# A selective scan in two layers: carry columns by transfer, D u by a diagonal matmul, 1/std turned later

## The chip, the cores and the metric

The kernel runs on one core of a Trainium2 chip. Five engines work side by side, each through its own queue of instructions in order: TensorE (matmuls, PE in the profile, with its weight loads as PEld), VectorE (DVE), ScalarE (ACT), GpSimd (POOL) and SyncE (SP), which here only issues transfers. The metric is the device time of one execution in microseconds (us), the median of several runs.

## What is computed

The reference has two layers over an input of 4 x 192 x 128 x 128 floats. Layer 1 (group norm, fractional Fourier transforms, small convolutions) is not touched by the change. Layer 2 takes most of the time. It is a state space block on sequences of 16384 tokens with 192 channels, 4 of them in the batch:

```python
seq = (seq - mu) * lax.rsqrt(var + LN_EPS) * ln_g + ln_b      # layer norm per token
xs, z = jnp.split(einsum('blc,ec->ble', seq, in_proj_w), 2)   # 384 inner channels each
u = silu(conv1d(xs, 4 taps, per channel))
dt, Bm, Cm = split(einsum('bld,kd->blk', u, x_proj_w))        # 16 states
dt = softplus(einsum('blr,dr->bld', dt, dt_proj_w) + dt_proj_b)
h[t] = h[t-1] * exp(dt[t] * A) + (dt[t] * u[t]) * B[t]        # 384 channels x 16 states
y[t] = sum over states (h[t] * C[t]) + u[t] * Dp
out = einsum('bld,cd->blc', y * silu(z), out_proj_w)
```

All in float32. The recurrence over t is what makes the work serial: h at the end of one stretch of tokens is the start of the next.

## The kernel before

Layer 2 (`layer1` in the code, which counts from 0) cuts each sequence into chunks of T = 512 tokens: 32 per batch entry, 128 in all. The 384 inner channels are NJ = 3 tiles (j) of 128 partitions. The 16 states are taken in pairs: 8 pairs per tile, 24 **groups** k = 0 to 23 per chunk (j = k // 8, sg = k % 8). One group is the unit of the main loop:

- VectorE scans two states (`tensor_tensor_scan`, L865), 128 x 512 each, into h. Between the scans it forms products dt u B of later groups (L816).
- ScalarE makes exp(dt A) for states ahead (L796).
- GpSimd multiplies h of the group by C (`hc`, L878), and in 8 of 24 groups also makes dt u B (`db`, L824).
- TensorE adds up hc over the states, three groups later, by turning it: 8 transposes of 128 x 128 into py in PSUM (`sums`, L891).

The tile h has 3 buffers: group k + 3 writes where group k was, so k must have been read by then.

The other work of layer 2 is spread over the groups. `front(n)` is a generator that does for one chunk all that comes ahead of the scans: norm, in-projection, convolution, SiLU, B and C, dt. It is started two chunks ahead, at group 14, and takes one step per group, so that two fronts are always under way: the older one ends at group 23, the newer one begins. A plain `yield` ends a step. What follows `yield MID` is issued between the two scans of that group, what follows `yield LATE` after both. The order of instructions on each engine is thus written out by hand; no scheduler moves them.

In the newer front the layer norm's 1/std per token comes out in columns (tokens on partitions) and is needed in rows. The path runs over these steps, with the group of the chunk in which each is issued:

- group 18, LATE: sums of squares `var` on TensorE (L630)
- group 19, LATE: square root on ScalarE, which needs a table load (L637)
- group 20: reciprocal on VectorE (L639), then its turn on TensorE (L641); between the scans the copy `rows` on ScalarE (L644)
- group 21, LATE: four matmuls on TensorE that spread each row over 96 partitions (`rb`, L649)
- group 22, between the scans: s times 1/std on VectorE (L654)
- group 23: the first in-projection of that front (L660)

The older front issues two in-projections for z among these (L660): one at group 20, ahead of the turn, and one at group 22.

At the end of each group ScalarE copies the last columns of h into `carry` (L876), for the same group of the next chunk. Once per tile j, in group sg = 1, it multiplies u by Dp in place (`skip`, L905). In group sg = 3 TensorE adds that into py by four transposes (`add_skip`, L910), after `sums` of the group three earlier; py has one buffer, which ScalarE empties into yt in group sg = 2 (`evacuate`, L900), so the first `sums` into the new py waits for that copy. yt is turned back (L920), and VectorE multiplies it with silu(z) (`gate`, L925) in group sg = 6.

SyncE issues the loads of B and C, spread over the partitions (`bc`, L770, 1 MB each, 8 per chunk, in groups 19 to 23 and 0 to 2), the store of B and C they are read from (`dbc`, L727), the load of x (L594) and the store of the result (L942).

Of the kernel before, what the change touches and what calls it, by code (L numbers as in the profile page):

```python
# [10 lines left out]
F32 = mybir.dt.float32  # L11
I32 = mybir.dt.int32
BF16 = mybir.dt.bfloat16
AF = mybir.ActivationFunctionType
ALU = mybir.AluOpType
# [12 lines left out]
NJ = DI // 128  # L28
NS = 16
RANK = 12  # L30
T = 512
# [11 lines left out]
def _bc(ap, axis, n):  # L43

    a = ap.unsqueeze(axis)
    shape = list(a.shape)
    shape[axis] = n
    return a.to_broadcast(shape)
# [455 lines left out]
def layer1(tc, xmid, out, st2, w, n_tok=S * S):  # L504

    nc = tc.nc
    B = len(xmid)
    NCHUNK = n_tok // T
    G = 2
# [6 lines left out]
    MID, LATE = "mid", "late"  # L516
    with ExitStack() as ctx:
        def pool(name, bufs, **kw):
            return ctx.enter_context(tc.tile_pool(name=name, bufs=bufs, **kw))

        cp = pool("l1c", 1)
# [13 lines left out]
        def const(name):  # L535
            src = w[name]
            t = cp.tile(list(src.shape), F32, name="c_" + name)
            nc.sync.dma_start(out=t, in_=src)
            return t

        wiT, ln_g, ln_b, xpT, dtT, dtb = (const(k) for k in ("wiT", "ln_g", "ln_b", "xpT", "dtT", "dtb"))
        cw, cb, dp, woT, A = (const(k) for k in ("cw", "cb", "dp", "woT", "A_log"))

        ident = cp.tile([128, 128], F32, name="ident")
# [17 lines left out]
        for m in range(2 * NJ):  # L562
            for t in range(2):
                nc.tensor.matmul(
                    ps[:, m : m + 1], wiT[:, t, m * 128 : (m + 1) * 128], ln_b[:, t : t + 1],
                    start=t == 0, stop=t == 1,
# [5 lines left out]
        nc.scalar.activation(A, A, AF.Exp)  # L572
        nc.vector.tensor_scalar(A, A, -1.0, None, ALU.mult)

        dcw = cp.tile([128, NJ, 4, 128], F32, name="dcw")
        for j in range(NJ):
            for k in range(4):
# [5 lines left out]
        def psum():  # L583
            return ps1.tile([128, 512], F32, name="ps")
# [4 lines left out]
        got = [{} for _ in range(total)]  # L589
# [9 lines left out]
        def front(i):  # L599

            b, ch = divmod(i, NCHUNK)
            g = got[i]
# [25 lines left out]
            for q in range(4):  # L628
                for t in range(2):
                    nc.tensor.matmul(  # L630
                        var[:, q : q + 1], sq[:, t, q * 128 : (q + 1) * 128], ones[0:CH, 0:1],
                        start=t == 0, stop=t == 1,
# [3 lines left out]
            rs = tp.tile([128, 4], F32, name="rs")  # L636
            nc.scalar.activation(rs, var[:, 0:4], AF.Sqrt, bias=eps, scale=1.0 / C)  # L637
            yield
            nc.vector.reciprocal(rs, rs)  # L639
            rt = psum()  # L640
            nc.tensor.transpose(rt[0:4, 0:128], rs, ident)  # L641
            yield MID
            rows = tp.tile([4, 128], F32, name="rows")
            nc.scalar.copy(rows, rt[0:4, 0:128])  # L644
            yield
            yield LATE
            rb = psum()
            for q in range(4):
                nc.tensor.matmul(  # L649
                    rb[0:CH, q * 128 : (q + 1) * 128], sel[:, q, :], rows, start=True, stop=True  # L650
                )
            yield
            yield MID
            nc.vector.tensor_tensor(s, s, _bc(rb[0:CH], 1, 2), ALU.mult)  # L654
            yield

# [25 lines left out]
            u, zs = g["u"], g["zs"] = {}, {}  # L682
# [92 lines left out]
        def dtu_copy(n, j):  # L775

            g = got[n]
            g["dp"] = psd.tile([128, T], F32, name="dp")
            nc.scalar.copy(g["dp"], g["dtu"][j])  # L779
# [19 lines left out]
        def early(i):  # L799

            if i < len(own):
                decay(own[i], scp.tile([128, T], F32, name="da"))

        def decay_there(s):

            if s < len(states) and s not in turns:
                decay(s, psa.tile([128, T], F32, name="op"))

        def product(s):


            if s in turns and states[s][1] % NG != BY_PE:
                n, k, q = states[s]
                g = got[n]
                dbs[s] = psa.tile([128, T], F32, name="op")
                nc.vector.tensor_tensor(dbs[s], g["dp"], g["bc", k % NG][:, 0, q, :], ALU.mult)  # L816
# [36 lines left out]
        def scans(pos, n, k, between):  # L853
            g = got[n]
            j, sg = divmod(k, NG)
            ch = n % NCHUNK
            if k == 0:
                g["carry"] = tp.tile([128, NJ, NS], F32, name="carry")
                g["before"], last["carry"] = last.get("carry"), g["carry"]
            db = g.pop(("db", k), None)  # L860
            h = scp.tile([128, G, T], F32, name="h", bufs=3)
            for q in range(G):
                st = sg * G + q
                s = G * pos + q
                nc.vector.tensor_tensor_scan(  # L865
                    h[:, q, :], das.pop(s), dbs.pop(s) if db is None else db[:, q, :],
                    0.0 if ch == 0 else g["before"][:, j, st : st + 1], ALU.mult, ALU.add,
                )
                product(s + 2)
                decay_there(s + 3)  # L870
                if q == 0:
                    turned_back(s + 3)
                    between()
                if s in turns:
                    early(turns[s] + AHEAD)
            nc.scalar.copy(g["carry"][:, j, sg * G : (sg + 1) * G], h[:, :, T - 1])  # L876
            hc = scp.tile([128, G, T], F32, name="hc", bufs=5)
            nc.gpsimd.tensor_tensor(hc, h, g["bc", sg][:, 1], ALU.mult)  # L878
            g["hc", k] = hc
# [19 lines left out]
            yt = g["yt", j] = op.tile([128, T // 128, 128], F32, name="yt")  # L899
            nc.scalar.copy(yt, g["py", j])  # L900

        def skip(n, j):

            u = got[n]["u"][j]
            nc.scalar.activation(u, u, AF.Identity, scale=dp[:, j : j + 1])  # L905

        def add_skip(n, j):

            for blk in range(T // 128):
                nc.tensor.matmul(  # L910
                    got[n]["py", j][:, blk, :], got[n]["u"][j][:, blk * 128 : (blk + 1) * 128], ident,
                    start=False, stop=False, is_transpose=True, skip_group_check=True,
                )

        def turn(n, j):
# [51 lines left out]
        with tc.manual_schedule():  # L967
            for i in range(min(2, total)):
                load_x(i)
            for _ in front(0):  # L970
                pass
            for sg in range(NG):
                load_bc(0, sg)
            dtu_copy(0, 0)
            inputs(*order[1])
            for at in range(AHEAD):
                early(at)
            for s in range(2):
                product(s)
            decay_there(2)  # L980


            start_front(1)
            for _ in range(NGR - FRONT):
                parts = {MID: [], LATE: []}
                step(fronts, parts)
                go_on(parts[MID] + parts[LATE])
            tails = []
            for pos, (n, k) in enumerate(order):
                j, sg = divmod(k, NG)  # L990
                if k == FRONT:
                    start_front(n + 2)
                if k == NGR - 2 and n + 1 < total:
                    assert len(fronts) == 1 + (n + 2 < total), fronts
                parts = {MID: [], LATE: []}
                step(tails, parts)

                before = n - (j == 0), (j - 1) % NJ
                if pos >= NG and sg == LAG + 3:
                    gate(*before)  # L1000
                if sg == BY_PE - 1:
                    turned_back(G * (pos + 1))
                if pos >= LAG and sg != LAG:
                    sums(*order[pos - LAG])
                if k == EARLY or sg == LAG - 1 and j < NJ - 1:
                    turned(n, NJ - 1 if k == EARLY else j)
                if sg == NG - 3 and pos + 3 < len(order):
                    m, q = order[pos + 3]
                    dtu_copy(m, q // NG)
                step(fronts, parts)  # L1010
                if pos >= NG and sg == LAG + 1:
                    turn(*before)
                if pos + 2 < len(order):
                    inputs(*order[pos + 2])

                def between():
                    go_on(parts[MID])
                    if sg == LAG and j < NJ - 1:
                        scale_pair(n, j)

                scans(pos, n, k, between)
                if pos >= NG and sg == LAG - 1:
                    evacuate(*before)
                go_on(parts[LATE])
                if sg == 1:
                    skip(n, j)
                if k == EARLY:
                    scale_pair(n, NJ - 1)
                if pos >= LAG and sg == LAG:
                    sums(*order[pos - LAG])  # L1030
                    add_skip(n, j)
                if k == LAG + 3 and n:
                    tails.append(finish(n - 1))
                if k == LAG + 8 and n + 2 < total:
                    load_x(n + 2)
                if k >= NGR - BCL and n + 1 < total:
                    load_bc(n + 1, k - (NGR - BCL))
                if k < NG - BCL and n:
                    load_bc(n, k + BCL)
            for at in order[-LAG:]:  # L1040
                sums(*at)
            evacuate(total - 1, NJ - 1)
            turn(total - 1, NJ - 1)
            gate(total - 1, NJ - 1)
            for _ in finish(total - 1):
                pass
# [139 lines left out]
```

## Time and profile before

Three runs took 11835.06 to 11841.85 us, median 11841.73. The profiled execution spans 11838.7 us. Layer 2 begins its chunks at about 1500 us.

| engine | busy us | share | instructions |
|---|---|---|---|
| TensorE | 9907.6 | 84% | 49034 |
| VectorE | 10772.0 | 91% | 11581 |
| ScalarE | 9108.1 | 77% | 17892 |
| GpSimd | 10080.6 | 85% | 4598 |

| what the change touches | busy us | count | mean ns |
|---|---|---|---|
| ScalarE, carry copies (L876) | 563.3 | 3072 | 188 |
| ScalarE, u times Dp (L905) | 278.5 | 384 | 725 |
| TensorE, D u into py (L910) | 300.6 | 1536 | 332 |
| VectorE, reciprocal (L639) | 22.8 | 128 | 178 |

A row of the timeline reads: start in us, duration in us, engine, line, operation, output <- inputs, output shape <- input shape, count of merged instructions, and in brackets the idle time of the engine just ahead with what ended it. Matmuls are pipelined and their ends are modelled, so how fast TensorE goes is better read from start to start. A row of the windows has the stretch, its length, then busy time (and instructions) of PE, PEld, DVE, ACT and POOL, the granted TensorE clock as a share of full speed, the busy share of the DMA engines and the GB/s they moved.

### The profile page before, as it was taken

Reading aid. Unit: us, or ns where it says so; the run is one execution under the profiler, and the core shown is the slowest. Engines: PE = TensorE matmul, PEld = TensorE weight load, DVE = VectorE, ACT = ScalarE, POOL = GpSimd, SP = SyncE. Lnnn points to the kernel's source line nnn. Section 1 sums busy time; section 2 is a strip of 40 time slices with the busy share of each in tenths; the row PEclk is TensorE's granted clock in tenths of the full one; section 3 lists DMA queues with packets and bytes.
Section 4 is the critical chain, followed back from the end, with each engine's and each line's share of the span. In section 5 each row is a group of like instructions: output and inputs, shape, how many; then the busy total and the mean of one; then the engine's idle time right before and its main releaser. Section 6 shows DMA issues by size and latency. Waiting matters only on the chain.

```text
span 11838.7 us, 147015 instructions
## 1 busy us (share of the span) xinstructions
PE 9907.6 (84%) x49034; PEld 6573.6 (56%) x49034; DVE 10772.0 (91%) x11581; ACT 9108.1 (77%) x17892; POOL 10080.6 (85%) x4598
## 2 busy tenths in 40 slices
PE   4777888888888888888888888888888888888887
PEld 2444355555555555555555555555555555555555
DVE  5565589999999999999999999999999999999999
ACT  2322178888888888888888888888888888888887
POOL 0000089999999999999999999999999999999999
PEclk8888689999999999999999999999999999999998
DMA  8787633333333333333333333333333333333332
GB/s 212 211 214 195 179 122 105 118 123 107 115 123 110 113 123 112 111 123 114 109 123 115 108 123 117 106 123 117 106 123 120 103 123 122 102 122 124 102 121 95
DMA packets 503761, 1490.33 MB, mean 126 GB/s; under 512 B 67889, under 2 KB 118774, under 8 KB 502486
## 3 DMA queue, kind: packets, MB, share of 16 engines
q1 hardware_dynamic: 482518, 1418.00, 37.1%
q0 software_dynamic: 13312, 50.34, 1.3%
q10 hardware_dynamic: 7168, 12.59, 0.3%
q8 instruction: 385, 6.31, 0.2%
q14 instruction: 378, 3.10, 0.1%
HBM read 1325.19 MB, written 155.32 MB: 125 GB/s over the span
## 4 chain that ended last, share of the span: by engine, by line
DVE 35%; ACT 27%; issue 23%; PE 9%; POOL 3%; DMA 2%; SPq 0%; ACTq 0%; DVEq 0%; POOLq 0%
DVE h L865 22%; DVE op L816 10%; ACT da L796 8%; ACT L796 4%; POOL hc L878 3%; PE py L891 2%; ACT dbT L840 2%; ACT op L796 2%; PE pr L471 1%; ACT dt L741 1%; PE ps L660 1%; ACT L741 1%; DMA xt<-in_x 1%; ACT xs L622 1%; ACT zs L690 1%
## 5 line engine op out<-in xcount | busy, mean ns | idle before, releaser
L878 POOL TENSOR_TENSOR hc<-h,bc 128x1024 f32<-128x1024 f32 x3072 | 7196.6, 2367 | 344.6 <-DVE h L865 268.9
L865 DVE TENSOR_TENSOR_SCAN h<-da,carry,op 128x512 f32<-128x512 f32 x3968 | 4932.1, 1263 | 1.3 <-DVE rs L639 0.3
L891 PE MATMUL py<-ident,hc 128*128 128x128 f32 x24576 | 3489.0, 291 | 720.1 <-ACT yt L900 679.9
L891 PEld LDWEIGHTS py<-ident,hc 128*128 128x128 f32 x24576 | 3057.4, 151 | 1716.9 <-POOL db L824 673.4
L796 ACT ACTIVATE da<-dt,c_A_log 128x512 f32<-128x512 f32 x4096 | 2806.0, 721 | 138.6 <-DVE h L865 114.2
L865 DVE TENSOR_TENSOR_SCAN h<-op,carry,db 128x512 f32<-128x512 f32 x1984 | 2510.7, 1266 | 101.5 <-ACT op L796 89.6
L824 POOL TENSOR_TENSOR db<-dtu,bc 128x1024 f32<-128x1024 f32 x1024 | 2418.9, 2362 | 5.6 <-DMA bc<-dbc 5.6
L816 DVE TENSOR_TENSOR op<-dp,bc 128x512 f32<-128x512 f32 x3328 | 2230.7, 670 | 33.3 <-ACT dp L779 33.3
L796 ACT ACTIVATE op<-dt,c_A_log 128x512 f32<-128x512 f32 x2048 | 1411.9, 690 | 818.3 <-DVE h L865 816.7
L660 PE MATMUL ps<-s,c_wiT 96*128 96x512 f32 x3072 | 1498.2, 611 | 12.8 <-ACT zs L690 8.2
L678 PE MATMUL ps<-xs,dcw 128*128 128x512 f32 x3072 | 1448.4, 601 | 0.0
L934 PE MATMUL ps<-yg,c_woT 128*96 128x512 f32 x1536 | 710.5, 598 | 190.9 <-DVE xm L940 190.9
L840 ACT ACTIVATE dbT<-ps,bT 128x128 f32<-128x128 f32 x3072 | 826.0, 373 | 0.0
L796 ACT ACT_TABLE_LOAD x636 | 816.0, 1283 | 11.2
L678 PEld LDWEIGHTS ps<-xs,dcw 128*128 128x128 f32 x3072 | 539.9, 193 | 466.5 <-issue 438.8
L660 PEld LDWEIGHTS ps<-s,c_wiT 96*128 96x128 f32 x3072 | 546.8, 199 | 438.9 <-issue 395.3
L477 POOL DMA_DIRECT2D xmid<-xt x64 | 42.6, 666 | 785.5 <-DVE xt L475 779.3
L876 ACT COPY carry<-h 128x2 f32<-128x2 f32 x3072 | 563.3, 188 | 23.1 <-DVE h L865 22.5
L934 PEld LDWEIGHTS ps<-yg,c_woT 128*96 128x96 f32 x1536 | 239.9, 163 | 557.6 <-issue 330.0
L630 PE MATMUL ps<-ones,xs 96*128 96x1 f32 x2048 | 345.5, 299 | 226.9 <-ACT dt L741 222.0
L745 POOL TENSOR_TENSOR dtu<-dt,u 128x512 f32<-128x512 f32 x384 | 476.6, 1268 | 29.1 <-ACT dt L741 29.1
L630 PEld LDWEIGHTS ps<-ones,xs 96*128 96x128 f32 x2048 | 334.6, 255 | 269.3 <-ACT dt L741 261.2
(173 smaller groups left out, 10771.0 us busy)
## 6 DMA issues: line engine op xcount, KB each, us to landing
bc<-dbc SPq DMA_DIRECT2D x1024, 1024.0 KB, 5.4
xt<-in_x SPq DMA_DIRECT2D x192, 768.0 KB, 9.1
xmid<-xt POOLq DMA_DIRECT2D x64, 768.0 KB, 6.7
xm<-xmid SPq DMA_DIRECT2D x128, 384.0 KB, 3.5
out<-xm SPq DMA_DIRECT2D x128, 384.0 KB, 3.0
d<-x ACTq DMA_DIRECT2D x64, 192.0 KB, 7.6
df<-u SPq DMA_DIRECT2D x16, 512.0 KB, 5.2
u<-df SPq DMA_DIRECT2D x16, 512.0 KB, 11.0
```

Of the source, the lines that this page charges most:

```text
L630: nc.tensor.matmul(var[:, q : q + 1], sq[:, t, q * 128 : (q + 1) * 128], ones[0:CH, 0:1], start=t == 0, stop=t == 1,)
L660: nc.tensor.matmul(pp, wiT[:, t, m * 128 : (m + 1) * 128], s[:, t, :], start=t == 0, stop=t == 1)
L678: nc.tensor.matmul(pc, dcw[:, j, k, :], xs[:, j, k : k + T], start=k == 0, stop=k == 3)
L796: nc.scalar.activation(da, got[n]["dt"][j], AF.Exp, scale=A[:, j, st : st + 1])
L816: nc.vector.tensor_tensor(dbs[s], g["dp"], g["bc", k % NG][:, 0, q, :], ALU.mult)
L824: nc.gpsimd.tensor_tensor(db, _bc(g["dtu"][j], 1, G), g["bc", sg][:, 0], ALU.mult)
L840: nc.scalar.activation(t[:, blk, :], g["tu", j][:, blk, :], AF.Identity, scale=g["bT"][:, blk, q : q + 1])
L865: nc.vector.tensor_tensor_scan(h[:, q, :], das.pop(s), dbs.pop(s) if db is None else db[:, q, :], 0.0 if ch == 0 else g["before"][:, j, st ...
L876: nc.scalar.copy(g["carry"][:, j, sg * G : (sg + 1) * G], h[:, :, T - 1])
L878: nc.gpsimd.tensor_tensor(hc, h, g["bc", sg][:, 1], ALU.mult)
L891: nc.tensor.matmul(py[:, blk, :], hc[:, q, blk * 128 : (blk + 1) * 128], ident, start=first, stop=sg == NG - 1 and q == G - 1 and blk == T ...
L934: nc.tensor.matmul(po[0:CH], woT[:, j, t * CH : (t + 1) * CH], g["yg", j], start=j == 0, stop=j == NJ - 1,)
```

## The change

Three edits, all in layer 2:

- The last columns of h go to `carry` by a transfer that SyncE issues, and no longer by a ScalarE copy. The aim is to relieve ScalarE.
- D u comes from one matmul with a diagonal of Dp (`ddp`, made once ahead of the loop) in place of a ScalarE product and a transpose. Two aims: to relieve ScalarE, and to leave u unchanged.
- The reciprocal moves behind the scans of group 20, so that VectorE doesn't stand at it. What follows moves with it: the turn to group 21, ahead of its scans; `rows` between the scans of group 21; `rb` to group 22, ahead of its scans, which puts it behind the older front's in-projection of that group in TensorE's queue; s times 1/std after the scans of group 22. The in-projection of group 23 stays where it was.

```diff
+        ddp = cp.tile([128, NJ, 128], F32, name="ddp")
+        for j in range(NJ):
+            nc.vector.tensor_scalar(ddp[:, j, :], ident, dp[:, j : j + 1], None, ALU.mult)
...
             nc.scalar.activation(rs, var[:, 0:4], AF.Sqrt, bias=eps, scale=1.0 / C)
             yield
+            yield LATE
             nc.vector.reciprocal(rs, rs)
+            yield
             rt = psum()
             nc.tensor.transpose(rt[0:4, 0:128], rs, ident)
             yield MID
             rows = tp.tile([4, 128], F32, name="rows")
             nc.scalar.copy(rows, rt[0:4, 0:128])
             yield
-            yield LATE
             rb = psum()
             for q in range(4):
                 nc.tensor.matmul(
                     rb[0:CH, q * 128 : (q + 1) * 128], sel[:, q, :], rows, start=True, stop=True
                 )
-            yield
-            yield MID
+            yield LATE
             nc.vector.tensor_tensor(s, s, _bc(rb[0:CH], 1, 2), ALU.mult)
...
-            nc.scalar.copy(g["carry"][:, j, sg * G : (sg + 1) * G], h[:, :, T - 1])
+            nc.sync.dma_start(out=g["carry"][:, j, sg * G : (sg + 1) * G], in_=h[:, :, T - 1])
...
-        def skip(n, j):
-
-            u = got[n]["u"][j]
-            nc.scalar.activation(u, u, AF.Identity, scale=dp[:, j : j + 1])
-
         def add_skip(n, j):
 
             for blk in range(T // 128):
                 nc.tensor.matmul(
-                    got[n]["py", j][:, blk, :], got[n]["u"][j][:, blk * 128 : (blk + 1) * 128], ident,
-                    start=False, stop=False, is_transpose=True, skip_group_check=True,
+                    got[n]["py", j][:, blk, :], got[n]["u"][j][:, blk * 128 : (blk + 1) * 128],
+                    ddp[:, j, :], start=False, stop=False, skip_group_check=True,
                 )
...
-                if sg == 1:
-                    skip(n, j)
```

## The prediction

> **What bounds the kernel now.** I read the waits first, then the windows, then the timeline of one chunk, engine by engine.
>
> Of the waits (engine, line, released by: us in total, times, longest) these matter to layer 2:
>
> ```profile
> DVE rs L639 <- ACT rs L637: 292.7, 128, 5.1
> POOL hc L878 <- DVE h L865: 268.9, 136, 18.7
> DVE h L865 <- ACT op L796: 97.1, 148, 2.7
> ```
>
> The windows give busy time per engine in 1000 us of steady layer 2:
>
> ```profile
> 6000.00:7000.00 1000.00, 853.58 (x4437) 581.29 (x4436) 959.38 (x1019) 850.47 (x1691) 967.29 (x437) 0.93 0.35 119
> ```
>
> VectorE is busy 959 us and GpSimd 967 us. A chunk is 80.45 us (L639 starts at 6017.53 and 6097.98), so VectorE idles 3.1 us per chunk and GpSimd 2.5. VectorE's idle time is two waits: 2.23 us for the square root ahead of L639, and 0.7 us for L796. GpSimd's idle time follows from the first: it catches up while VectorE stands. If all waits went, GpSimd would set the pace at 80.45 - 2.5 = 77.9 us.
>
> The timeline round that wait, VectorE:
>
> ```profile
> 6095.07 0.67 DVE L816 TENSOR_TENSOR op<-dp,bc 128x512 f32<-128x512 f32 x1
> 6097.98 0.18 DVE L639 RECIPROCAL rs<-rs 128x4 f32<-128x4 f32 x1 [2.23 <-ACT rs L637]
> 6103.97 0.67 DVE L925 TENSOR_TENSOR yg<-ps,zs 128x512 f32<-128x512 f32 x1
> 6105.73 1.19 DVE L654 TENSOR_TENSOR s<-s,ps 96x1024 f32<-96x1024 f32 x1
> ```
>
> ScalarE, which has no idle time from 6072 to 6098:
>
> ```profile
> 6091.05 0.74 ACT L905 ACTIVATE u<-u,c_dp 128x512 f32<-128x512 f32 x1
> 6094.43 0.57 ACT L900 COPY yt<-py 128x512 f32<-128x512 f32 x1
> 6097.68 0.27 ACT L637 ACTIVATE rs<-ps,eps 128x4 f32<-128x4 f32 x1
> ```
>
> TensorE, from the evacuation of py on:
>
> ```profile
> 6095.14 1.94 PE L891 MATMUL py<-ident,hc 128*128 128x128 f32 x8 [2.72 <-ACT yt L900]
> 6096.88 1.06 PE L910 MATMUL py<-ident,u 128*128 128x128 f32 x4
> 6097.73 1.91 PE L891 MATMUL py<-ident,hc 128*128 128x128 f32 x8
> 6099.44 1.98 PE L660 MATMUL ps<-s,c_wiT 96*128 96x512 f32 x4
> 6101.26 0.28 PE L641 MATMUL ps<-ident,rs 128*4 128x128 f32 x1
> ...
> 6103.64 1.11 PE L649 MATMUL ps<-rows,sel 4*96 4x128 f32 x8
> 6104.68 1.09 PE L891 MATMUL py<-ident,hc 128*128 128x128 f32 x8
> 6105.61 1.88 PE L660 MATMUL ps<-s,c_wiT 96*128 96x512 f32 x4
> 6107.33 1.04 PE L891 MATMUL py<-ident,hc 128*128 128x128 f32 x8
> ```
>
> From 6095.14 to the end of L649 at 6104.75 TensorE has no pause. So a second chain runs beside the first: yt, 9.6 us of TensorE, then L654, which finds its sums ready with 1.0 us to spare.
>
> [...] the eight turns of L891 take 1.74 us to the next start at 6095.14 and 0.93 at 6104.68. [...] here four turns are four records, four f32 matmuls of L649 are eight of like spacing, so I take a factor of two. [...] In the packet records of this trace 4 bytes take 9 ns in the median. [...]
>
> **The change part by part.**
>
> *Carry by transfer.* ScalarE loses 24 copies per chunk; each delays the next instruction by 0.09 us, together 2.2 us. VectorE waited for them 4.2 us in all. New: the h tile is free only when the transfer has landed. Lower bound of landing: 1.6 us (dbc store). Upper: it follows a bc load issued one group earlier, which lands 7.1 us after issue at worst; groups are about 3.3 us apart, so 7.1 + 0.4 issue - 3.3 + 0.2 = 4.4 us. VectorE needs the tile again two groups later, about 6 us. I take no wait. Behind a carry issue in SP's order stand the bc loads: they now start at the end of their group's scans, land some 6 us later, and the earliest reader (L824, after the product hc two groups on) comes about 9 us later: no wait. Transfer engines: 17 packets of about 10 ns, 0.2 us per group beside a DMA share of 0.35.
>
> *D u by a diagonal.* ScalarE loses three L905, 2.2 us per chunk, one of them ahead of yt. TensorE gets four more records three times a chunk: 0.43 us each at full clock, 0.85 at half. The one in group 19 lies on the chain above. Setup of ddp: three small VectorE products, nothing beside 11.8 ms.
>
> *Reciprocal after the scans of group 20.* VectorE gets there 3.5 us after 6095.65, the square root is over by 6098: the 2.23 us go.
>
> *The rest of the turn one group later.* This is where it is decided. L649 now stands behind L891 of group 19 and the older front's L660: 0.93 + 1.72 us more of TensorE ahead of it, and L654 comes after both scans of group 22.
> - TensorE: L905 and six carry copies gone before yt give 0.7 + 0.5 = 1.2 us, so the chain starts at 6093.9. It lasts 9.6 + 0.85 + 0.93 + 1.72 = 13.1 us and ends at 6107.0.
> - VectorE is free of the group before at 6095.65. Then scan, product, scan, product (3.53), reciprocal 0.1, two scans 2.36, gate 0.58, two scans 2.37: it reaches L654 at 6104.6.
> - New wait: 2.4 us. The same working for the four other neighbouring chunks (reciprocals at 6017.5, 6178.4, 6259.4, 6339.8; chains of 9.1 without a wait for VectorE, 10.35, 9.2, 9.86) gives 1.65, 3.2, 1.8, 2.8. Mean 2.36: what differs is how long the half clock lasts.
> - TensorE's pause ahead of the chain shrinks from about 1.8 to 1.0 us, so the clock may come back sooner. An estimate: 0.3 to 0.6 us less half clock, worth half of it, 0.15 to 0.3. I take 2.15 us, range 1.2 (the clock soon back) to 3.0 (half clock throughout).
>
> Behind L654 stand the scans of group 23, so the wait costs VectorE its full length. The 0.7 us for L796 stay: ScalarE starts that stretch from the dp copy, which waits for a VectorE product.
>
> Sum per chunk: -2.23 + 2.15 = -0.1 us; over 127 chunks -10 us, and a few more for carry waits: **11,830 us**, no change that can be told.
>
> **Rivals.**
> 1. *The wait goes and GpSimd becomes the bound.* For: GpSimd needs only 77.9 us, and ScalarE is relieved of 4.4 us per chunk. Against: even at full clock the chain is about 10.6 us, from 6093.9 to 6104.5, just where VectorE arrives; it needs a TensorE that never slows there. If so: 2.2 to 2.5 us in 127 chunks, 11,530 to 11,560. Half of it: about 11,690.
> 2. *The new wait is longer than the old.* For: chunks with a long half clock (3.2 and 2.8 above), and the added f32 records run just then. Against: the shorter pause. At 2.8 us: 0.57 x 127 = +72, 11,915.
> 3. *Carry transfers hold h.* For: 3072 transfers on the queue of the bc loads, which moved 359 GB/s in single 3 us windows. Against: landing at most 4.4 us of 6. If each of the eight groups with a bc load lost 0.2 us: 1.6 x 127 = +200, 12,030.
>
> **How the numbers follow.** The wait moves and keeps its size within 0.4 us: 0.60 (below 11,818 in 0.24, within 0.2% in 0.21, above 11,866 in 0.15). It mostly goes (rival 1 or half of it): 0.21. Rival 2: 0.14. Rival 3: 0.05. Faster 0.45, same 0.21, slower 0.34. The range runs from half of rival 1 to just past rival 2, which leaves out about 0.1 on either side: 11,690 to 11,925.
>
> **What would show it.** Right: no wait ahead of the reciprocal; one of about 2 us ahead of the product with 1/std (L654 of now), released by TensorE's spreading of 1/std (L649 of now); GpSimd idle about as before; ScalarE near 72% busy; no transfer among VectorE's releasers. Wrong: that product waits under 1 us (the clock came back, or TensorE was earlier than I count), or scans wait for carry transfers, or bc is late for the products.

## The result, and the profile after

The changed kernel took 11751.58 us (median of 4 runs, 11749.99 to 11753.17) against 11841.79 (4 runs of the kernel before). The ratio is 0.9925, with a 95% interval from 0.9908 to 0.9942: 90 us faster, where 12 had been forecast.

A chunk (mean distance of the reciprocal from one chunk to the next) takes 79.84 us, before 80.54. The difference of 0.70 us times 127 is 89 us, so the whole change lies in the steady chunks of layer 2. All figures per chunk below are means over 110 or more chunks.

The longest waits of VectorE in the kernel before, between 1700 and 11400 us (120 chunks; each row has the total in us, the number of waits and the longest):

```profile
DVE rs L639 <- ACT rs L637: 268.8, 120, 2.6
DVE h L865 <- ACT op L796: 89.5, 139, 1.0
DVE h L865 <- ACT carry L876: 3.7, 11, 0.7
```

The waits of VectorE, and the longest of GpSimd, in the changed kernel in the same stretch (121 chunks). L657 is the product with 1/std, L653 the spreading of 1/std, L868 the scan:

```profile
DVE s L657 <- PE ps L653: 210.7, 121, 2.3
DVE h L868 <- issue: 80.0, 121, 0.7
...
DVE h L868 <- DMA carry<-h: 1.0, 1, 1.0
...
POOL hc L881 <- DVE h L868: 190.4, 370, 1.2
```

The reciprocal, which waited 2.24 us per chunk, has no row left. Now the product waits, once in every chunk, for 1.74 us. One wait has taken the other's place, and is half a microsecond shorter. The scan's wait of 0.7 us is still there; the profile no longer names a releaser for it. In 121 chunks one scan waited for a carry transfer.

The same 1000 us of the windows as in the prediction:

```profile
6000.00:7000.00 1000.00, 873.55 (x4624) 607.78 (x4622) 967.49 (x1027) 804.50 (x1362) 978.11 (x440) 0.94 0.39 116
```

VectorE and GpSimd rise by 8 and 11 us, as the shorter chunk demands. ScalarE falls from 850 to 805. Between 3000 and 11000 us GpSimd's idle time went from 2.54 us per chunk to 1.78: it still catches up while VectorE waits.

VectorE's timeline from the reciprocal to the product:

```profile
6061.76 0.17 DVE L643 RECIPROCAL rs<-rs 128x4 f32<-128x4 f32 x1
6061.85 2.43 DVE L868 TENSOR_TENSOR_SCAN h<-da,carry,op 128x512 f32<-128x512 f32 x2
6064.18 0.67 DVE L923 TENSOR_TENSOR yg<-ps,zs 128x512 f32<-128x512 f32 x1
6064.77 2.45 DVE L868 TENSOR_TENSOR_SCAN h<-da,carry,op 128x512 f32<-128x512 f32 x2
6068.28 1.22 DVE L657 TENSOR_TENSOR s<-s,ps 96x1024 f32<-96x1024 f32 x1 [1.07 <-PE ps L653]
```

And TensorE's, to be read from start to start, from the first sums into the emptied py to the spreading:

```profile
6056.71 1.94 PE L894 MATMUL py<-ident,hc 128*128 128x128 f32 x8
6058.44 1.29 PE L908 MATMUL py<-ddp,u 128*128 128x128 f32 x8
6059.56 1.04 PE L894 MATMUL py<-ident,hc 128*128 128x128 f32 x8
6060.44 1.88 PE L663 MATMUL ps<-s,c_wiT 96*128 96x512 f32 x4
...
6064.45 1.04 PE L894 MATMUL py<-ident,hc 128*128 128x128 f32 x8
6065.33 1.88 PE L663 MATMUL ps<-s,c_wiT 96*128 96x512 f32 x4
6067.14 1.11 PE L653 MATMUL ps<-rows,sel 4*96 4x128 f32 x8
```

The spreading ends at 6068.25 and the product starts at 6068.28. Ahead of the spreading stand the sums of group 19 (6064.45) and the older front's z (6065.33), 2.7 us together; `rows`, which it reads, was there by 6064.5:

```profile
6064.22 0.25 ACT L649 COPY rows<-ps 4x128 f32<-4x128 f32 x1 [0.97 <-PE ps L646]
```

So the product waits for the place in TensorE's queue, not for data.

The transfers (KB each, median us from issue to landing):

```profile
bc<-dbc SPq DMA_DIRECT2D x1024, 1024.0 KB, 5.9
...
carry<-h SPq DMA_DIRECT2D x3072, 1.0 KB, 1.9
```

A carry lands after 1.9 us, while its tile is wanted again after some 6. The longest of the 1150 landings that the trace has took 6.0 us, more than the 4.4 that the forecast had as its upper bound, and one scan waited for a carry. Of 268 carries that were issued while a bc load was under way none landed ahead of that load, and their median was 3.5 us: so far the trace bears out what the prediction expected, a carry behind a running load. The bc loads land half a microsecond later than before (5.4), which costs almost nothing: GpSimd waited for them 4.6 us in these 121 chunks, VectorE not at all.

### The profile page after: what moved, and what is told of

Same layout as the page of the kernel before. It is cut to its first block, busy times and chain, and to the rows that moved or that the text cites. A ratio compares the mean times of both kernels' runs of the same rounds, so it can differ in the third digit from the quotient of the medians.

```text
span 11750.5 us, 153548 instructions
## 1 busy us (share of the span) xinstructions
PE 9994.0 (85%) x50570; PEld 6788.1 (58%) x50570; DVE 10759.5 (92%) x11584; ACT 8606.6 (73%) x14436; POOL 10087.8 (86%) x4598
## 4 chain that ended last, share of the span: by engine, by line
DVE 42%; ACT 20%; PE 19%; issue 12%; DMA 4%; POOL 1%; DVEq 1%; SPq 0%; ACTq 0%; POOLq 0%
DVE h L868 29%; DVE op L819 10%; PE py L894 5%; ACT da L799 5%; ACT op L799 4%; PE ps L663 3%; ACT dbT L843 2%; ACT L799 2%; PE pr L471 2%; PE py L908 2%; ACT dt L744 1%; DMA xt<-in_x 1%; ACT L744 1%; DMA bc<-dbc 1%; PE ps L653 1%
## 5 line engine op out<-in xcount | busy, mean ns | idle before, releaser
L868 DVE TENSOR_TENSOR_SCAN h<-da,carry,op 128x512 f32<-128x512 f32 x3968 | 4945.7, 1271 | 2.3 <-issue 0.5
L868 DVE TENSOR_TENSOR_SCAN h<-op,carry,db 128x512 f32<-128x512 f32 x1984 | 2522.3, 1271 | 84.2 <-issue 82.2
L663 PE MATMUL ps<-s,c_wiT 96*128 96x512 f32 x3072 | 1468.5, 601 | 38.4 <-DVE s L657 38.4
L681 PE MATMUL ps<-xs,dcw 128*128 128x512 f32 x3072 | 1424.3, 592 | 0.2 <-ACT xs L676 0.2
L908 PE MATMUL py<-ddp,u 128*128 128x128 f32 x3072 | 536.0, 333 | 0.0
L908 PEld LDWEIGHTS py<-ddp,u 128*128 128x128 f32 x3072 | 511.1, 251 | 0.0
```

The lines of the kernel that those rows point to most:

```text
L663: nc.tensor.matmul(pp, wiT[:, t, m * 128 : (m + 1) * 128], s[:, t, :], start=t == 0, stop=t == 1)
L681: nc.tensor.matmul(pc, dcw[:, j, k, :], xs[:, j, k : k + T], start=k == 0, stop=k == 3)
L868: nc.vector.tensor_tensor_scan(h[:, q, :], das.pop(s), dbs.pop(s) if db is None else db[:, q, :], 0.0 if ch == 0 else g["before"][:, j, st ...
L908: nc.tensor.matmul(got[n]["py", j][:, blk, :], got[n]["u"][j][:, blk * 128 : (blk + 1) * 128], ddp[:, j, :], start=False, stop=False, skip ...
```

## The experiments

Eight kernels ran in two groups. The kernel before took 11837.32 us beside the first four and 11838.43 beside the others. Three theories stood: (A) the change moves the wait from the reciprocal to the product, because the spreading stands late in TensorE's queue, and ScalarE's relief, which starts that chain earlier, makes the new wait a little shorter; (B) the later turn is the gain; (C) ScalarE's relief is all of the gain.

### 1. The spreading put right behind the rows

Against the changed kernel, the spreading moves from group 22 to the middle of group 21:

```diff
             nc.scalar.copy(rows, rt[0:4, 0:128])
-            yield
             rb = psum()
             ...
+            yield
             yield LATE
```

> The changed kernel, but the four matmuls that spread 1/std (rb) are issued right behind the copy of the rows, between the scans of group 21, and so ahead of the sums of group 19 and of the older front's z projection in TensorE's queue. Moved wait (my theory: the 1.74 us ahead of s times 1/std in the changed kernel is TensorE's chain from the emptying of py): the chain is shorter by 0.93 + 1.72 us less some 0.7 us in which TensorE waits for the rows, so the wait falls to 0.2 us or so on average; 1.5 us in 127 chunks less, 11,560 us, and no less than about 11,525, where GpSimd has no idle time left. Rival (the wait belongs to the rows on ScalarE or to the half clock whatever stands ahead): the wait stays at 1.5 us or more, 11,730 to 11,760 us.

Measured: 11518.36 us (11515.38 to 11527.72), ratio to the kernel before 0.9733 (0.9720 to 0.9746). Its waits of VectorE between 1700 and 11400 us, all of over 3 us in sum, and then its window from 3000 to 11000 us:

```profile
DVE h L868 <- issue: 82.6, 126, 0.7
```

```profile
3000.00:11000.00 8000.00, 7048.03 (x37856) 4907.03 (x37855) 7924.82 (x8414) 6601.70 (x11178) 7993.27 (x3594) 0.94 0.40 120
```

The product's wait is gone, and GpSimd is busy for 7993 of 8000 us: it is the bound now, with a chunk of 77.98 us. The wait was one of order in a queue. The time is 42 us below the expected 11,560 and 7 us below the floor that was named; the chunk comes within 0.1 us of the 77.9 us that GpSimd was said to need. This is the fastest kernel of the study.

### 2. The later turn alone

The kernel before with the turn's edit (reciprocal, turn, spreading and product later), and nothing else:

```diff
             yield
+            yield LATE
             nc.vector.reciprocal(rs, rs)
+            yield
             rt = psum()
             ...
-            yield LATE
             rb = psum()
             ...
-            yield
-            yield MID
+            yield LATE
             nc.vector.tensor_tensor(s, s, _bc(rb[0:CH], 1, 2), ALU.mult)
```

> The kernel before with the later reciprocal and turn alone: carry copies and the product u Dp stay on ScalarE. Moved wait: without ScalarE's relief TensorE's chain starts 0.9 us later against VectorE, and is 0.4 us shorter without the added f32 records; the new wait is about 2.3 us, as long as the old one, so 11,842 us within 25. Rival (the turn alone makes the gain): 11,750 us. Rival (ScalarE's relief makes it): 11,842 as well; the run without the turn tells those two apart.

Measured: 11907.55 us (11901.66 to 11911.55), ratio 1.0059 (1.0047 to 1.0072): slower by 70 us, where 11,842 within 25 was expected: a miss. VectorE's waits between 1700 and 11400 us (here L654 is the product, L925 the product with silu(z), L865 the scan):

```profile
DVE s L654 <- PE ps L650: 261.2, 119, 2.3
DVE h L865 <- ACT op L796: 83.9, 123, 1.0
DVE yg L925 <- PE ps L920: 58.5, 89, 1.5
```

The product's wait, 2.19 us in each of 119 chunks, is as long as that of the reciprocal had been. What the expectation lacked is the third row. Without ScalarE's relief the chain on TensorE starts 1.0 us later, and its earlier part, yt turned back, is late for `gate` too: 58.5 / 119 = 0.49 us a chunk. Theory B falls.

### 3. ScalarE's relief alone

The changed kernel with the turn where it was before (the edit of experiment 2, undone):

```diff
             yield
-            yield LATE
             nc.vector.reciprocal(rs, rs)
-            yield
             rt = psum()
             ...
+            yield LATE
             rb = psum()
             ...
-            yield LATE
+            yield
+            yield MID
             nc.vector.tensor_tensor(s, s, _bc(rb[0:CH], 1, 2), ALU.mult)
```

> The changed kernel with reciprocal and turn put back to where they were: carry by transfer and D u by the diagonal alone. Moved wait: VectorE waits ahead of the reciprocal again, 0.3 to 0.4 us less than before as ScalarE comes to the square root that much earlier: 11,795 us (11,780 to 11,815). Rival (ScalarE's relief makes the whole gain): 11,750. Rival (the turn makes it all): 11,842.

Measured: 11753.60 us (11749.66 to 11757.97), ratio 0.9930 (0.9917 to 0.9942), the time of the changed kernel. VectorE's longest waits between 1700 and 11400 us:

```profile
DVE rs L642 <- ACT rs L640: 219.4, 121, 1.8
DVE h L868 <- issue: 81.2, 124, 1.0
```

The reciprocal waits 1.81 us and not 2.24: without copies and products ahead of it ScalarE ends its square root 0.43 us earlier relative to VectorE. The expectation had 0.3 to 0.4 of that. It missed by 41 us, because the chunk lost 0.67 us in all: the scan's wait fell too, from 0.74 to 0.67, the waits for carry copies (0.03) went, and VectorE's busy time fell by 0.11 us a chunk. Why the last fell is not shown. In time theory C, the rival's 11,750, fits: the relief alone gives 84 of the 90 us, within noise all of them. But the relief's worth depends on the turn: 84 us without it (11837.32 to 11753.60), about 156 with it (11907.55 to 11751.58). The turn as placed costs 70 us without the relief and nothing with it, as then its wait is as long as the one it removes (1.74 and 1.81 us). So theory A says rightly where the wait went, and C where the time came from.

### 4. The spreading early, without the relief

Experiment 1 upon the kernel before, with the carry and D u as they were:

```diff
+            yield LATE
             nc.vector.reciprocal(rs, rs)
+            yield
             rt = psum()
             ...
             nc.scalar.copy(rows, rt[0:4, 0:128])
-            yield
-            yield LATE
             rb = psum()
             ...
             yield
-            yield MID
+            yield LATE
             nc.vector.tensor_tensor(s, s, _bc(rb[0:CH], 1, 2), ALU.mult)
```

> The kernel before with the later reciprocal and turn alone, and with rb issued right behind the copy of the rows (as in the run rb_early); carry copies and u Dp stay on ScalarE. Moved wait: TensorE's chain starts 1.0 us later against VectorE than with ScalarE relieved and lasts 9.4 us; it ends some 0.2 us ahead of VectorE on average, with 0.2 to 0.4 us of waits in the chunks with a long half clock. Left are the 0.74 us for L796. Period 78.6 us at most, 11,585 us (11,550 to 11,610): most of the gain of rb_early comes without any relief of ScalarE. Rival (relief is needed, since the turn alone was slower than before): 11,680 us or more.

Measured: 11586.91 us (11583.69 to 11593.60), ratio 0.9788 (0.9775 to 0.9802), as expected. VectorE's waits between 1700 and 11400 us, all of over 2 us in sum:

```profile
DVE h L865 <- ACT op L796: 87.5, 131, 1.0
DVE yg L925 <- PE ps L920: 4.4, 6, 1.2
```

Those for reciprocal and product are both gone; the chunk is 78.51 us. So the later turn is worth 250 us when the spreading stands ahead of the two other works in TensorE's queue, and loses 70 when it stands behind them. The relief adds 69 us to the well-placed version (11586.91 to 11518.36).

### 5. The carry on ScalarE again

The changed kernel with one line undone:

```diff
-            nc.sync.dma_start(out=g["carry"][:, j, sg * G : (sg + 1) * G], in_=h[:, :, T - 1])
+            nc.scalar.copy(g["carry"][:, j, sg * G : (sg + 1) * G], h[:, :, T - 1])
```

> The changed kernel with the carry copies back on ScalarE. Moved wait: six copies ahead of the emptying of py start TensorE's chain 0.5 us later, so the wait ahead of s times 1/std is 2.2 us instead of 1.74, and 0.1 to 0.3 us more at other places: 11,825 us (11,800 to 11,850). Rival (the copies were hidden, VectorE waited for them 4 us in all): 11,755 us.

Measured: 11799.57 us (11792.42 to 11803.67), ratio 0.9967 (0.9955 to 0.9979), at the fast edge of what was expected. The carry by transfer is worth 48 us in this kernel. The waits of product and scan:

```profile
DVE s L657 <- PE ps L653: 228.4, 121, 2.3
DVE h L868 <- ACT op L799: 84.8, 124, 1.0
```

The product waits 1.89 us for 1.74, the scan 0.70 for 0.66. That is 0.19 of the 0.36 us by which the chunk is longer. Most of the rest is VectorE's busy time, 77.49 us a chunk for 77.35; why it grows with copies on ScalarE was not settled.

### 6. u times Dp on ScalarE again

The changed kernel with `skip` back in group sg = 1, and transposes of u in `add_skip`:

```diff
+        def skip(n, j):
+
+            u = got[n]["u"][j]
+            nc.scalar.activation(u, u, AF.Identity, scale=dp[:, j : j + 1])
...
-                    got[n]["py", j][:, blk, :], got[n]["u"][j][:, blk * 128 : (blk + 1) * 128],
-                    ddp[:, j, :], start=False, stop=False, skip_group_check=True,
+                    got[n]["py", j][:, blk, :], got[n]["u"][j][:, blk * 128 : (blk + 1) * 128], ident,
+                    start=False, stop=False, is_transpose=True, skip_group_check=True,
...
+                if sg == 1:
+                    skip(n, j)
```

> The changed kernel with u Dp back on ScalarE and four transposes with the identity on TensorE. Moved wait: the chain starts 0.5 to 0.7 us later and is 0.4 to 0.7 us shorter, so the two nearly cancel: 11,765 us (11,745 to 11,800). Rival (the ScalarE product costs its length): 11,840 us. Rival (the f32 records cost, as in plain_turns, and the ScalarE product is free): 11,670 us.

Measured: 11773.11 us (11763.43 to 11777.57), ratio 0.9944 (0.9931 to 0.9956), as expected. The edit is worth 22 us. The product's wait is a little longer than the changed kernel's 210.7 us:

```profile
DVE s L654 <- PE ps L650: 218.0, 121, 2.3
```

The chain starts 0.61 us later without the edit, and is 0.52 shorter; so with it most of the relief is paid back in the chain's length, by the f32 records and a clock that is slow for 0.17 us more.

The two parts of the relief don't add up: undone one at a time they cost 48 and 22 us, undone together (experiment 2 against the changed kernel) about 156. Only then is yt late for `gate`, for 0.49 us a chunk; with one part left that wait is 0.03 us or less.

### 7. Transposes, and no product on ScalarE either

The changed kernel with plain transposes of u into py, the factor Dp and the tile `ddp` left out:

```diff
-                    got[n]["py", j][:, blk, :], got[n]["u"][j][:, blk * 128 : (blk + 1) * 128],
-                    ddp[:, j, :], start=False, stop=False, skip_group_check=True,
+                    got[n]["py", j][:, blk, :], got[n]["u"][j][:, blk * 128 : (blk + 1) * 128], ident,
+                    start=False, stop=False, is_transpose=True, skip_group_check=True,
```

> The changed kernel, but u is added into py by four transposes with the identity as before and not by four f32 matmuls with the diagonal: the factor Dp is left out. Moved wait: four records fewer on TensorE's chain ahead of rb, 0.43 us at full clock to 0.85 at half: the wait falls from 1.74 to 0.9 to 1.3 us, 11,645 to 11,695 us. Rival (real matmuls bring the clock back sooner than transposes and pay for themselves): 11,745 us or more.

Measured: 11667.37 us (11662.23 to 11681.18), ratio 0.9858 (0.9845 to 0.9872), as expected: f32 matmuls for D u in place of plain transposes cost 84 us. The product waits 1.2 us for 1.74, and the chain is 11.64 us long for 12.31:

```profile
DVE s L654 <- PE ps L650: 145.2, 122, 2.3
```

### 8. TensorE's pause ahead of the chain filled

The changed kernel with the turns of B's rows made twice, in the group ahead of the chain. The author's guess, which no trace had shown, was that the clock would come back sooner if TensorE were better filled there:

```diff
-            for blk in range(T // 128):
+            for blk in list(range(T // 128)) * 2:
```

> The changed kernel with the four transposes of group 19 that turn the B rows issued twice, the same values to the same place, to fill TensorE's pause ahead of the chain. Moved wait with the clock as a term of it: the pause shrinks, [...] the half clock after the chain's start gets 0.5 to 1 us shorter: wait 0.2 to 0.5 us less, 11,690 to 11,725 us. Rival (only the order of work counts): the four records fit into the pause, no change, 11,750; or they reach beyond it and delay the chain by up to 0.5 us: 11,800 us.

Measured: 11772.37 us (11768.97 to 11783.24), ratio 0.9946 (0.9933 to 0.9958): slower than the changed kernel by 21 us, and a miss. The product's wait:

```profile
DVE s L657 <- PE ps L653: 229.0, 121, 2.3
```

The mean pause ahead of the chain fell from 0.94 to 0.56 us, and TensorE's time at half clock between 2000 and 11300 us stayed at 1204.9 us to the digit (granted clock between 3000 and 11000 us: 0.94 in both kernels). The chain started 0.23 us later, for the turns were in its way, and the wait grew by 0.15 us (229.0 against 210.7 in 121 chunks), 19 us in all.

When the clock changes is in its records. In the traces of the kernel before and of the changed kernel every stretch of half clock (235 and 270 of them), but for the last, which ends with the execution, is a whole multiple of 3.4133 us long, and within 0.02 us they all begin and end on one grid of that spacing. Windows of the changed kernel cut along it, around the chain that was shown above:

```profile
6045.26:6048.67 3.41, 1.82 (x13) 0.98 (x13) 3.41 (x4) 3.41 (x10) 3.41 (x3) 1.00 0.10 19
6048.67:6052.08 3.41, 2.40 (x12) 2.00 (x10) 3.41 (x5) 3.38 (x5) 3.21 (x2) 0.50 0.10 3
...
6055.50:6058.91 3.41, 3.41 (x17) 3.20 (x18) 3.41 (x5) 2.81 (x6) 3.41 (x3) 0.50 0.05 3
6058.91:6062.32 3.41, 3.41 (x21) 2.40 (x21) 3.41 (x6) 3.37 (x5) 3.41 (x3) 1.00 0.74 235
```

After a window in which TensorE was busy for 1.82 of 3.41 us (the number behind the length) the clock is 0.50; here it comes back after one in which it was busy throughout. The chain's start at 6056.71 stands within the slow window, and its first 2.2 us, to the edge at 6058.91, are slow. What decides at an edge is left open. Windows with up to 1.9 us idle kept full clock as well. Between 2000 and 11300 us 45 of the 212 returns of the clock came after windows with 0.33 to 0.76 us idle, while 28 windows with less than 0.1 us idle were followed by another slow one. In that stretch each of the 212 falls came after a window with 0.75 to 2.4 us idle.

## Why the prediction was right, and where it was off

**The wait that moves.** Right. The wait ahead of the reciprocal went, a new one came ahead of the product, released by the spreading, and the two works in front of it are the named ones. Experiments 1 and 4 show that the order in the queue is its cause. ScalarE's share, 73%, is near the 72 that was named. But "no change that can be told" did not come: the interval of the ratio lies below 1, and the result lies in the branch below 11,818, which had been given 0.24.

**Its size.** Here the numbers were off: 2.15 us forecast, 1.74 measured, worth 52 of the 78 us by which the forecast missed. With D for the time at which VectorE is done with group 19:

| | forecast | measured |
|---|---|---|
| chain starts | D - 1.75 | D - 1.5 |
| its length, us | 13.1, less some 0.2 by the clock | 12.31 |
| VectorE reaches the product | D + 8.95 | D + 9.1 |
| wait, us | 2.15 | 1.74 |

The mis-sized step is the length, 0.59 us under the 12.9 that were forecast. In the wait a part of that is hidden, by luck: the chain starts 0.25 us later than forecast, which VectorE's arrival, 0.15 us later, makes up for only in part. The forecast put 0.85 + 0.93 + 1.72 = 3.5 us on the chain and took 0.2 off for the clock; measured it grew by 2.56, from 9.75. Its parts, from start to start:

| part of the chain, us | before | after |
|---|---|---|
| first sums | 1.73 | 1.73 |
| D u | 0.85 | 1.54 |
| sums of group 17 | 1.50 | 1.20 |
| first z | 1.97 | 1.75 |
| sums of group 18 | 1.02 | 0.87 |
| four turns in all | 1.57 | 1.42 |
| sums of group 19, older z | not in it | 0.87 + 1.81 |
| spreading | 1.11 | 1.11 |

- D u was priced as if added work at half clock cost double. Each by itself does: in the changed kernel D u's records are 0.11 us apart at full clock and 0.21 at half. But in the clock's records the slow stretch ends on an edge of the 3.41 us grid, so what the added records use of it is not used by the sums behind them. By this estimate they cost their full-clock price, 0.43 us. Experiment 7 bears it out: without them the chain is 0.67 us shorter, 0.28 of it because the clock is slow for 0.55 us less there, which leaves 0.39.
- The clock: "0.3 to 0.6 us less half clock, worth half of it". Measured 0.57 less (4.37 to 3.80), worth 0.28. The size was right, and so was the pause (forecast 1.8 to 1.0, mean 1.60 to 0.94). But the reason, a fuller TensorE bringing the clock back sooner, was the author's guess, and experiment 8 did not bear it out: 0.38 us less pause, 1204.9 us at half clock as before. What shortened the slow stretch is not shown, so that the size came out right is in part luck.
- The rest, 2.56 - (0.43 + 0.87 + 1.81 - 0.28) = -0.27 us, lies in the sums of group 18 and the turns, which took 1.02 and 1.57 us in the old chain though the clock was back by then (0.87 and 1.42 after). That these are small waits, which the longer queue hides, is a reading that no run tested.

**The relief.** Forecast 1.2 us for the chain's start, measured 1.0: 0.38 by the carry copies (0.5 forecast) and 0.61 by D u (0.7), from experiments 5 and 6.

**What was costed at nothing.** Carry transfers hold next to nothing (one wait of 1.0 us in 121 chunks): right, and rival 3 falls; DMA share 0.39. The scan's wait "stays 0.7": it fell from 0.74 to 0.66. VectorE's busy time per chunk fell by 0.10 us (77.45 to 77.35), and waits for carry copies, 0.03, went. Together some 0.2 us, about 25 us in all, which the sum lacked.

**Rivals.** Rival 1 (the wait goes, GpSimd the bound at 11,530 to 11,560) did not come, but experiment 1 reached its state at 11,518. Its argument against itself, that even a fast chain ends just when VectorE arrives, holds for the order as placed. Rival 2's longer wait did not come even without the relief: in experiment 2 the product waits 2.19 us, the reciprocal had waited 2.24, and what makes that kernel slower is the 0.49 us ahead of `gate`.

## What to carry to other kernels

When an instruction is moved later in a hand-ordered program, look at what then stands ahead of it in its engine's queue: here two works of 2.7 us, not its data, decided whether the same edit gained 250 us or lost 70. Compare the moved chain's end with the time at which its reader arrives, chunk by chunk, before pricing the wait that was removed. And where the records of the clock show a slow stretch that ends by time, as here on a grid of 3.41 us, price work added in it at full speed: D u's records cost about 0.4 us here, not 0.85. Last, undo the parts of a change one by one and together: here one of three brought nothing as placed, and could have brought the most.

## What the runs showed of the hardware

- An f32 matmul of 128 x 128 by 128 columns made two records, 0.11 us apart at full clock and 0.21 at half, a transpose of the same shape one: D u went from 1536 to 3072 records.
- In the changed kernel, between 2000 and 11300 us, TensorE's clock fell to half 212 times, each time after a window of 3.41 us in which TensorE had been idle for 0.75 to 2.4 us.
- A transfer of two columns (256 elements of 4 bytes) took 272 packets (835,584 more of under 512 bytes over 3072 transfers), 17 for each of the 16 DMA engines on average, landed in 1.9 us in the median, and with 24 in a chunk the DMA share rose from 0.34 to 0.39.
